# Moving one expert tile into the embedding, and small sums from VectorE to GpSimd, in a fused vision-tower layer

## The chip, the cores and the metric

The kernel runs on one core of a Trainium2 chip. The metric is the device time of one execution in microseconds (us). TensorE is called PE in the profile, VectorE DVE, ScalarE ACT, GpSimd POOL, and SyncE, which only issues transfers here, SP.

## The reference

The input x has the shape 4 x 64 x 512 x 64 (batch, channel, time, variable). Three stages follow each other; all is float32.

```python
# tokenizer: windows of 16 steps, stride 8, a real FFT of each, one linear layer
patches = xp[:, :, idx, :]                          # 64 windows of each variable
xf = rfft(patches, norm='ortho')
h = concat(xf.real, xf.imag) @ W.T                  # 4 x 4096 tokens of width 256

# retention layer on norm(h)
t = layernorm(h)
u = layernorm(t, g1, b1)
q, k, v = u @ Wq.T + bq, u @ Wk.T + bk, u @ Wv.T + bv
mem_t = decay * mem_{t-1} + k_t * v_t               # along the 4096 tokens
r = t + q * mem
h = h + r + (relu(layernorm(r, g2, b2) @ W1.T + b1) @ W2.T + b2)

# mixture of experts on norm(h): 8 experts, the best 2 for each token
t = layernorm(h)
p = softmax(t @ router.T); the two largest, scaled to sum 1, are the weights
h = h + t + sum over the chosen e of weight_e * (gelu(t @ w1[e] + b1[e]) @ w2[e] + b2[e])
```

## The kernel before, in words

**Blocks.** The 16,384 tokens are 32 blocks of 512 (four times 128). The main loop runs over blocks i from 0 to 30 and works on three of them at once: `new` is block i (embedding, q, k, v, retention), `mid` is block i-1 (the layer's MLP, whose 1024 columns are eight tiles of 128), `old` is block i-2 (router, scattering of its rows to the experts). The last block is treated after the loop.

**Order.** On TensorE, VectorE, ScalarE and SP the instructions stand in the order in which the program's text makes them; a step that is written earlier is queued earlier. GpSimd's order is left to the framework's scheduler. [...]

**The embedding** (`embed`, a generator that the loop advances by `next`) takes five products of differences of x. Products 1 and 2 go to one PSUM tile, which ScalarE copies to `ab` (line 423). Products 3 and 0 share another, and VectorE combines both into the four rows of `h` (line 420). Product 4 completes the last row. Statistics follow, GpSimd computes the norm's factors `rstd` (lines 288 to 293) by powers, and VectorE applies them (`zz`, line 297). `add_offsets` adds the MLP's second bias to `h` on GpSimd (line 454); `sum_up` adds the retention's result `z` to `h` on VectorE (line 648). `first_norm` makes `z` on ScalarE (line 459).

**Turning a block.** [...]From block 6 on a block is turned by a transfer: its floats are split into two 16-bit halves (`planes`, two ScalarE copies, line 330), SP issues a transposing transfer (`turned` or `turned_first`, line 340), and four copies join the halves to `hT` (line 349). In the earlier blocks TensorE transposes `zz` instead (line 310). `split1` and `features1` do this for the first norm, `split2` and `features2` for the norm before the MLP, `turn3` and `join3` for the router's tokens.

**Seven products for eight.** From block 7 on the MLP's two-by-two products are made of seven smaller ones with mixed sums of the input (`mix_normed`, `mix_tokens`; VectorE, lines 536 to 539). `mlp_group` works in steps between which the loop puts other work; three groups go in turn and the fourth, `rest`, later. q, k and v (`products`, called by `qkv`) are made in the same way from block 1 on: a first round of products, ScalarE copies into the fixed PSUM tiles `sums`, then rounds that add to them.

**Expert tiles.** Rows that go to one expert are collected in tiles of 256. A tile has six steps: `load` and `weigh` (SP fetches rows and the expert's weights, 641 KB), `turn` (two ScalarE copies to `xT`, line 1075), `enter` (first product, line 1082, and gelu, line 1090), `leave` (second product, line 1099), `sums` (VectorE adds the bias and scales, GpSimd adds the rows to the output in DRAM by two indirect transfers, line 1128). In each slot one tile enters and the tile before it leaves. Weights have four buffers, the PSUM pool `tm` has three, handed out in turn; a product into `tm` waits until the buffer of three uses before has been read. Four tiles run in a block of the steady part.

**Retention and residual.** `scan` multiplies k by v (line 614), runs the recurrence (line 615) and multiplies by q (`ret`, line 625). `residual` turns `ret` back on TensorE (line 636), adds it to `z` (line 639), takes statistics and computes the next norm's factors on VectorE in `factors_here`: an estimate by bits and three rounds of three small instructions (lines 276 to 282). The result, `zz`, is what `split2` splits.

**Routing.** `choose` finds both experts of each token, `place` counts the destinations and computes the row weights (`weights`), `scatter` sends the rows by eight indirect transfers on GpSimd (line 888); the later ones wait for given products of TensorE. `take` then lists the full tiles in some 21 tiny VectorE instructions; it stands between the request of the MLP norm's factors on GpSimd and their use in `tok`.

Of the kernel before, what the change touches and what calls it, by code (L numbers as in the profile page):

```python
# [12 lines left out]
F32 = mybir.dt.float32  # L13
# [23 lines left out]
def vit_tower_kernel(  # L37
# [160 lines left out]
    taken = const.tile([P, E], F32)  # L198
    nc.gpsimd.memset(taken, 0.0)
# [121 lines left out]
    class Turn:  # L321
# [5 lines left out]
        def split_steps(self, src, name="turned"):  # L327
            planes = one.tile([P, TT, 2 * D], U16, name="planes")
            for i, half in enumerate(halves(src)):
                nc.scalar.copy(planes[:, :, i * D : (i + 1) * D], half)  # L330
                if i:
                    self.start([planes.rearrange("p t d -> p (t d)")], name)
                yield
# [34 lines left out]
    class Block:  # L368
# [34 lines left out]
        def embed(self):  # L403
# [32 lines left out]
            scaled(h[3], c, 4.0 / 3, q, ALU.subtract)  # L436
            for t in range(TT - 1):
                norm.stats(self.h, t)
# [14 lines left out]
        def add_offsets(self):  # L453
            nc.gpsimd.tensor_tensor(self.h, self.h, mb2_sb.unsqueeze(1).to_broadcast([P, TT, D]), ALU.add)  # L454
# [86 lines left out]
        def products(self, which, first, to, order):  # L541
# [15 lines left out]
            def half(n):  # L557
                src = g[:, n, :]
# [6 lines left out]
            else:  # L565
                ps = p_tm.tile([P, 2, HALF], F32, name="tm")
            nc.tensor.matmul(ps[:, 0, :], lhsT=w11, rhs=a[:, :HALF], start=True, stop=True)
            nc.tensor.matmul(ps[:, 1, :], lhsT=t1, rhs=s1, start=True, stop=True)
            nc.scalar.copy(g, ps[:, 0:1, :].to_broadcast([P, 2, HALF]))
            p5 = three.tile([P, HALF], F32, name="p5")  # L570
            biased(p5, ps[:, 1, :], 1)
            yield
            add(0, w21, b[:, :HALF])
            add(1, t2, s2)
            biased(*half(0), 0)
# [15 lines left out]
            biased(*half(1), 0)  # L591
# [55 lines left out]
        def sum_up(self):  # L647
            nc.vector.tensor_tensor(self.h, self.h, self.z, ALU.add)

# [189 lines left out]

        def weights(self, diff, second):  # L840
# [19 lines left out]
        def place(self, at_once=True):  # L860
# [16 lines left out]
            self.weights(self.row.bitcast(F32)[:, :, DIFF], self.row.bitcast(F32)[:, :, SECOND])  # L877
# [49 lines left out]
    def take(n, block, writes):  # L927
# [5 lines left out]
        nc.vector.tensor_tensor(full, cnt, first[:, :E], ALU.subtract)  # L933
        if n == NS:
            nc.vector.tensor_scalar(full, full, float(S - 1), None, ALU.add)
        whole = small.tile([P, E], I32, name="whole")
        nc.vector.tensor_copy(whole, full)
        nc.vector.tensor_scalar(whole, whole, S.bit_length() - 1, None, ALU.arith_shift_right)
        nc.vector.tensor_copy(full, whole)

        nc.vector.tensor_tensor(full, full, taken, ALU.subtract)
        upto = small.tile([P, E + 1], F32, name="upto")
        nc.vector.memset(upto[:, 0:1], 0.0)
        nc.vector.tensor_tensor_scan(upto[:, 1:], ones_e, full, 0.0, ALU.mult, ALU.add)

        base = small.tile([P, E + 1], F32, name="base")
        nc.vector.tensor_tensor(base[:, :E], taken, upto[:, :E], ALU.subtract)
        nc.vector.tensor_scalar(base[:, E:], upto[:, E:], -1.0, None, ALU.mult)
        nc.vector.scalar_tensor_tensor(base, base, float(S), first, ALU.mult, ALU.add)

        shape = [P, k, E]
        past = one.tile([P, KMAX, E], F32, name="past")[:, :k, :]
# [7 lines left out]
        def along(to, of):  # L960

            step = small.tile([P, E], F32, name="step")
            nc.vector.tensor_tensor(step, of[:, 1:], of[:, :E], ALU.subtract)
            steps = one.tile([P, KMAX, E], F32, name="steps")[:, :k, :]
            nc.vector.tensor_tensor(steps, past, step.unsqueeze(1).to_broadcast(shape), ALU.mult)
# [10 lines left out]
        along(row, base)  # L976
        nc.vector.scalar_tensor_tensor(row, tile_f[:, :k], float(S), row, ALU.mult, ALU.add)
        done = None
        if n < NS:
            nc.vector.tensor_scalar(table[:, 1, :], row, base[:, 0:1], None, ALU.add)  # L980
# [606 lines left out]
```

## Time and profile before

| what | value |
|---|---|
| median of three runs | 2175.86 us (2172.4 to 2176.06) |
| the profiled execution, span | 2172.28 us, 2170.5 us |
| TensorE busy | 2075.3 us (96%) |
| VectorE busy | 1752.8 us (81%) |
| ScalarE busy | 1203.7 us (55%) |
| GpSimd busy | 963.1 us (44%) |
| steady block, embedding to embedding | some 63.4 us (1523.75 to 1587.16 is one) |
| granted TensorE clock, mean | 0.993 |

The profile comes from one execution. A line of its timeline has the start in us from the span's beginning, the duration in us, engine, source line, operation, tiles written and read, shapes, and in brackets the idle time of the engine before it and what ended it. A line of the waits names who waited for whom: us in total, times, longest us. PE and PEld are TensorE's products and its weight loads, which run beside each other; the end of a product is modelled. An fp32 product of 256 columns shows as two instructions.

### The profile page before, as it was taken

The numbers are of one execution on the slowest core, as the hardware profiler recorded it, in microseconds if no ns is written. First come the engines' busy times: TensorE is split into PE (matmuls) and PEld (weight loads), VectorE is DVE, ScalarE is ACT, GpSimd is POOL, SyncE is SP. The second block draws the span as 40 slices with busy tenths as digits, with TensorE's granted clock in tenths as the row PEclk, the third lists the DMA queues.
The fourth block names the chain that finished last, engine by engine and source line by source line (L and its number), as shares of the span: only waits on it lengthen the run. The fifth ranks groups of instructions, "written<-read, shape, count | busy, mean of one in ns | idle before, by whom it ended". The sixth has DMA issues, their size and how long they took to land.

```text
span 2170.5 us, 32402 instructions
## 1 busy us (share of the span) xinstructions
PE 2075.3 (96%) x9618; PEld 1671.4 (77%) x9618; DVE 1752.8 (81%) x5344; ACT 1203.7 (55%) x2350; POOL 963.1 (44%) x800
## 2 busy tenths in 40 slices
PE   8999999999999999999999999999999999899998
PEld 5776677877888777788877788887778888776776
DVE  7778888888888888888888888888888889768554
ACT  2344445765555675555567555556655556643443
POOL 1133334444455444445544444454445455335444
PEclk9999999999999999999999999999999999999999
DMA  4032246666576666567676656667665675768653
GB/s 138 8 116 65 84 107 135 133 146 135 127 159 145 151 125 149 132 137 158 145 150 127 146 127 146 157 141 153 128 145 129 146 157 139 137 173 197 104 74 49
DMA packets 424529, 283.32 MB, mean 131 GB/s; under 512 B 355104, under 2 KB 391072, under 8 KB 420256
## 3 DMA queue, kind: packets, MB, share of 16 engines
q1 hardware_dynamic: 373424, 208.35, 41.6%
q0 software_dynamic: 49632, 67.39, 17.0%
q10 hardware_dynamic: 1296, 5.52, 0.8%
q8 instruction: 75, 1.23, 0.2%
q14 instruction: 102, 0.84, 0.1%
HBM read 118.36 MB, written 86.52 MB: 94 GB/s over the span
## 4 chain that ended last, share of the span: by engine, by line
PE 44%; DVE 27%; DMA 11%; ACT 7%; issue 5%; POOL 4%; POOLq 0%; DVEq 0%; SPq 0%; ACTq 0%
PE tm L716 11%; PE sums L552 8%; PE mm L1082 6%; PE sums L357 6%; DMA turned<-planes 4%; DMA turned_first<-planes 4%; PE tm L1099 4%; DVE st L268 4%; DVE h L420 3%; ACT planes L330 3%; PE tm L414 2%; DVE zz L297 2%; ACT hT L349 2%; DMA out<-y,xg 2%; POOL rstd L293 2%
## 5 line engine op out<-in xcount | busy, mean ns | idle before, releaser
L1128 POOL DMA_INDIRECT out<-y,xg x226 | 387.5, 1715 | 441.8 <-DVE y L1118 217.4
L716 PE MATMUL tm<-w_sb,aT 128*128 128x256 f32 x2048 | 455.7, 381 | 0.0
L716 PEld LDWEIGHTS tm<-w_sb,aT 128*128 128x128 f32 x2048 | 388.2, 191 | 57.2 <-DVE z L639 4.6
L888 POOL DMA_INDIRECT xbuf<-row,to x248 | 262.1, 1057 | 169.2 <-DVE ks L588 88.9
L330 ACT COPY planes<-zz 128x1024 uint16<-128x1024 uint16 x100 | 99.6, 1042 | 341.9 <-DVE zz L297 299.3
L1099 PE MATMUL tm<-w,ge 128*128 128x256 f32 x1008 | 248.2, 390 | 36.2 <-ACT ab L423 36.2
L414 PE MATMUL tm<-wu,xv 128*128 128x256 f32 x1280 | 282.5, 379 | 0.0
L414 PEld LDWEIGHTS tm<-wu,xv 128*128 128x128 f32 x1280 | 242.7, 190 | 32.7
L1082 PE MATMUL mm<-xT,w 128*128 128x256 f32 x1008 | 241.9, 383 | 6.6 <-ACT xT L1075 4.5
L1099 PEld LDWEIGHTS tm<-w,ge 128*128 128x128 f32 x1008 | 187.8, 192 | 74.7 <-ACT ab L423 45.5
L288 POOL TENSOR_SCALAR rstd<-mv 128x4 f32<-128x4 f32 x62 | 42.0, 677 | 435.1 <-DVE mv L269 396.7
L1082 PEld LDWEIGHTS mm<-xT,w 128*128 128x128 f32 x1008 | 192.8, 192 | 37.1 <-ACT xT L1075 5.6
L1075 ACT COPY xT<-xh 128x512 uint16<-128x512 uint16 x262 | 181.7, 765 | 21.2 <-DMA xh<-xbuf 14.8
L1090 ACT ACTIVATE ge<-mm,w 128x256 f32<-128x256 f32 x252 | 105.5, 473 | 102.4 <-PE mm L1082 81.3
L349 ACT COPY hT<-turned 128x512 uint16<-128x512 uint16 x100 | 65.9, 757 | 141.9 <-DMA turned<-planes 141.9
L1116 DVE TENSOR_TENSOR y<-tm,w 128x512 f32<-128x512 f32 x126 | 87.1, 691 | 50.3 <-PE tm L1099 46.9
L357 PE MATMUL sums<-hT,w_sb 128*128 128x512 f32 x256 | 112.8, 592 | 0.0
L389 DVE TENSOR_TENSOR xv<-xb 128x512 f32<-128x512 f32 x160 | 104.2, 684 | 4.1 <-DMA xb<-in_x 4.1
L268 DVE BATCH_NORM_STATS2 st<-h 128x6 f32<-128x256 f32 x256 | 104.8, 409 | 3.3
L552 PE MATMUL sums<-hT,wqkv_sb 128*128 128x256 f32 x360 | 107.1, 379 | 0.0
L454 POOL TENSOR_TENSOR h<-h,mb_sb 128x1024 f32<-128x1024 f32 x32 | 90.7, 2835 | 23.9 <-ACT z L459 23.8
L297 DVE TENSOR_SCALAR zz<-h,mv,rstd 128x256 f32<-128x256 f32 x128 | 44.2, 409 | 67.2 <-POOL rstd L293 67.2
(265 smaller groups left out, 4168.1 us busy)
## 6 DMA issues: line engine op xcount, KB each, us to landing
w<-in_wex SPq DMA_DIRECT2D x111, 641.5 KB
xb<-in_x SPq DMA_DIRECT2D x32, 1040.0 KB
out<-h SPq DMA_DIRECT2D x31, 512.0 KB
bank<-in_wex ACTq DMA_DIRECT2D x8, 641.5 KB
xbuf<-row,to POOLq DMA_INDIRECT x248, 2.5
out<-y,xg POOLq DMA_INDIRECT x226, 5.5
xh<-xbuf SPq DMA_TRANSPOSE x131
xg<-xbuf SPq DMA_DIRECT2D x131, 4.0 KB
```

Source lines behind the costliest of these rows:

```text
L268: nc.vector.bn_stats(self.st[:, t, :], src[:, t, :])
L330: nc.scalar.copy(planes[:, :, i * D : (i + 1) * D], half)
L349: copy(to[:, 1 - i], self.turned[:, :, i, k, :])
L357: nc.tensor.matmul(ps, lhsT=w[:, k, ts(m, P)], rhs=rhs[:, k, :], start=k == 0, stop=k == KD - 1)
L414: nc.tensor.matmul(ps[:, n, :], lhsT=xv[:, i, j, :], rhs=wu[:, i, j, :], start=j == 0, stop=j == J - 1)
L552: nc.tensor.matmul(g[:, n, :], lhsT=lhsT, rhs=rhs, start=False, stop=True, skip_group_check=True)
L716: last_product[0] = nc.tensor.matmul(ps[:, i, :], lhsT=self.aT[:, k, ts(u * 2 + i, P)], rhs=w2_sb[:, k, :], start=k == 0, stop=k == KH - 1,)
L888: write = nc.gpsimd.indirect_dma_start(out=xbuf, out_offset=bass.IndirectOffsetOnAxis(ap=self.to[:, c, t : t + 1], axis=0), in_=self.row[: ...
L1075: nc.scalar.copy(halves[:, :, :, 1 - i], self.xh[:, i * KD : (i + 1) * KD, :])
L1082: nc.tensor.matmul(ps[:, m, :], lhsT=self.w[:, k * D + m * P : k * D + (m + 1) * P], rhs=self.xT[:, k, :], start=k == 0, stop=k == KD - 1,)
L1099: last_product[0] = nc.tensor.matmul(ps[:, c, :], lhsT=self.ge[:, k, ts(c, P)], rhs=w[:, (2 + k) * D : (3 + k) * D], start=k == 0, stop=k ...
L1128: add = nc.gpsimd.indirect_dma_start(out=out, out_offset=bass.IndirectOffsetOnAxis(ap=number[:, c, :], axis=0), in_=y[:, c, :], in_offset= ...
```

## The change

It reorders the loop's steps and moves some small work between engines:

- In blocks from 7 on, one tile's `enter` stands between the embedding's first two products and the next two, and the other tile's `leave` after these; `features2` follows the tile's entry. Before, the tile stood behind the whole embedding, and `features2` ahead of it. `split1` moves ahead of the last step of three MLP groups, the third tile's entry ahead of the fourth group's third step.
- `h + z` moves from VectorE to GpSimd, into `add_offsets`, which is called in the next block's pass, behind its embedding. For the last two blocks both sums are on VectorE.
- The row weights of `place` move to GpSimd (a power in place of the reciprocal).
- `take` has five fewer VectorE instructions: rounding by adding and subtracting a large number takes the place of two conversions and a shift.
- The first norm's split has one half on VectorE and one on ScalarE.
- The first round of q, k and v copies half as much, and its second round adds to the first product in place.
- `weigh` follows each tile's `sums` at once (`summed`); `turn` of a tile moves to other places.

The core of the diff:

```diff
@@ const
-    taken = const.tile([P, E], F32)
-    nc.gpsimd.memset(taken, 0.0)
...
+    nc.gpsimd.tensor_scalar(lower, first[:, :E], 1.0 / S, (S - 1) / (2.0 * S), ALU.mult, ALU.add)
+    minus = const.tile([P, TT], F32)
+    nc.gpsimd.memset(minus, -1.0)
@@ Turn.split_steps
-                nc.scalar.copy(planes[:, :, i * D : (i + 1) * D], half)
+                copy = nc.scalar.copy if i or name == "turned" else nc.vector.tensor_copy
+                copy(planes[:, :, i * D : (i + 1) * D], half)
@@ Block.add_offsets, sum_up
         def add_offsets(self):
+            nc.gpsimd.tensor_tensor(self.h, self.h, self.z, ALU.add)
             nc.gpsimd.tensor_tensor(self.h, self.h, mb2_sb.unsqueeze(1).to_broadcast([P, TT, D]), ALU.add)
...
         def sum_up(self):
             nc.vector.tensor_tensor(self.h, self.h, self.z, ALU.add)
+            nc.vector.tensor_tensor(self.h, self.h, mb2_sb.unsqueeze(1).to_broadcast([P, TT, D]), ALU.add)
@@ Block.products (q, k, v)
-            nc.tensor.matmul(ps[:, 0, :], lhsT=w11, rhs=a[:, :HALF], start=True, stop=True)
             nc.tensor.matmul(ps[:, 1, :], lhsT=t1, rhs=s1, start=True, stop=True)
-            nc.scalar.copy(g, ps[:, 0:1, :].to_broadcast([P, 2, HALF]))
+            nc.tensor.matmul(ps[:, 0, :], lhsT=w11, rhs=a[:, :HALF], start=True, stop=True)
             p5 = three.tile([P, HALF], F32, name="p5")
             biased(p5, ps[:, 1, :], 1)
+            nc.scalar.copy(g[:, 1, :], ps[:, 0, :])
             yield
-            add(0, w21, b[:, :HALF])
             add(1, t2, s2)
-            biased(*half(0), 0)
+            nc.tensor.matmul(ps[:, 0, :], lhsT=w21, rhs=b[:, :HALF], start=False, stop=True, skip_group_check=True)
+            biased(*half(0, ps), 0)
             nc.scalar.copy(g[:, 0, :], g[:, 1, :])
@@ Block.weights_there, called by place
+            share = small.tile([P, TT], F32, name="share")
+            nc.gpsimd.tensor_scalar(share, self.ex, 1.0, None, ALU.add)
+            nc.gpsimd.tensor_tensor(share, share, minus, ALU.pow)
+            nc.gpsimd.tensor_tensor(second, share, self.ex, ALU.mult)
+            nc.gpsimd.tensor_tensor(diff, share, second, ALU.subtract)
@@ take
-        nc.vector.tensor_tensor(full, cnt, first[:, :E], ALU.subtract)
+        nc.vector.scalar_tensor_tensor(full, cnt, 1.0 / S, lower, ALU.mult, ALU.subtract)
...
-        nc.vector.tensor_copy(whole, full)
-        nc.vector.tensor_scalar(whole, whole, S.bit_length() - 1, None, ALU.arith_shift_right)
-        nc.vector.tensor_copy(full, whole)
-
-        nc.vector.tensor_tensor(full, full, taken, ALU.subtract)
...
+        nc.vector.tensor_scalar(full, full, ROUND, None, ALU.add)
+        nc.vector.scalar_tensor_tensor(full, full, ROUND, taken, ALU.subtract, ALU.subtract)
@@ new helper
+    def summed():
+        advance("sums", at["leave"])
+        advance("weigh", at["leave"] + 4 + len(spare))
@@ main loop, start of a block's pass
-            embed = new.embed()
-            if seven:
-                mid.features2()
-                advance("turn", min(at["enter"] + 2, at["load"]))
-            next(embed)
-            if seven:
-                mid.mix_normed()
-            elif i > 1:
+            embed = new.embed(seven)
+            next(embed)
+            if i > 1 and not seven:
+                mid.features2()
+            tile_steps = iter(())
+            if seven:
+                tile_steps = slot_halves(known, load=False, turn=0, further=1, sums=False)
+                next(tile_steps, None)
                 mid.features2()
             if old:
                 old.rows()
                 old.turn3()
             next(embed)
+            if seven:
+                run(tile_steps)
+                mid.mix_normed()
+                next(embed)
...
-            if mid:
-                mid.sum_up()
+            summed()
...
             next(embed, None)
-            if at["enter"]:
-                slot(known, load=False, further=seven, sums=not seven)
+            if mid:
+                mid.add_offsets()
+            if at["enter"] and not seven:
+                slot(known, load=False)
@@ main loop, MLP groups, blocks from 7 on
-                for _ in range(3):
+                for n in range(3):
+                    if n == 2:
+                        advance("turn", min(at["enter"] + 2, at["load"]))
+                        new.split1()
...
-                new.split1()
-                next(tokens)
...
                 new.features1()
                 new.mix_tokens()
+                tile_steps = slot_halves(known, sums=False, turn=0)
+                next(tile_steps, None)
+                next(rest)
                 old.logits()
-                next(rest)
-                advance("sums", at["leave"])
@@ main loop, q, k, v (blocks from 7 on: the tile leaves between the first and the second round)
-                run(chain(rest, *groups[:3]))
+                run(rest)
+                if seven:
+                    old.choose()
+                next(qkv)
+                run(chain(*groups[:3]))
                 if i >= EARLY:
                     run(ahead)
-                next(qkv)
-                tile_steps = slot_halves(known, sums=False)
-                next(tile_steps, None)
+                run(tile_steps)
                 next(qkv)
                 if old:
                     writes = old.place(at_once=False)
                     old.scatter(1)
-                run(tile_steps)
-                if old:
                     old.scatter(2, last_product[0])
...
                 new.first_norm()
-                new.add_offsets()
@@ main loop, end of a block's pass
+            if i == NS - 1:
+                slot(known)
+            if at["enter"]:
+                advance("weigh", at["enter"] + AHEAD - 2)
+                advance("load", at["enter"] + AHEAD - 1)
...
                 new.split2()
+                summed()
```

## The prediction

> **What bounds the kernel now.** I read the page's engine totals first, then who waited for whom on TensorE, then the timeline of one repeating block (1450 to 1514 us), then that of an early block.
>
> ```profile
> PE 2075.3 (96%) x9618; PEld 1671.4 (77%) x9618; DVE 1752.8 (81%) x5344; ACT 1203.7 (55%) x2350; POOL 963.1 (44%) x800
> ```
>
> TensorE (PE) is the bound: only its stalls can be won. From the 256-column products' usual distance from start to start (216 ns, and likewise for the other shapes) I count some 180 us of stalls in all, weight loads made late after a wait included. The waits name the largest:
>
> ```profile
> PE tm L1099 <- ACT ab L423: 36.2, 23, 3.3
> PE tm L636 <- DVE ret L625: 10.9, 6, 2.4
> PE tm L676 <- DVE h L420: 6.2, 22, 0.3
> PE sums L676 <- ACT sums L689: 5.5, 24, 0.3
> PE sums L552 <- DVE ks L588: 3.9, 4, 2.7
> PE mm L1082 <- DMA w<-in_wex: 2.1, 1, 2.1
> ```
>
> The first happens once in each block from the seventh on. The timeline shows how:
>
> ```profile
> 1454.10 0.67 DVE L639 TENSOR_TENSOR z<-tm,z 128x512 f32<-128x512 f32 x1
> ...
> 1456.88 0.17 DVE L280 TENSOR_TENSOR st<-rstd 128x4 f32<-128x4 f32 x1
> 1456.97 0.97 POOL L888 DMA_INDIRECT xbuf<-row,to  x1 [0.30 <-issue]
> ...
> 1458.67 1.38 DVE L297 TENSOR_SCALAR zz<-z,mv,rstd 128x256 f32<-128x256 f32 x4
> ...
> 1460.09 1.99 ACT L330 COPY planes<-zz 128x1024 uint16<-128x1024 uint16 x2 [11.95 <-DVE zz L297]
> ...
> 1461.68 1.61 POOL L1128 DMA_INDIRECT out<-y,xg  x1 [3.74 <-DVE y L1118]
> ...
> 1467.67 2.63 ACT L349 COPY hT<-turned 128x512 uint16<-128x512 uint16 x4 [5.60 <-DMA turned<-planes]
> ...
> 1471.41 0.57 ACT L423 COPY ab<-tm 128x512 f32<-128x512 f32 x1
> 1472.01 0.76 DVE L420 SCALAR_TENSOR_TENSOR h<-ab 128x256 f32<-128x256 f32 x2 [3.52 <-ACT ab L423]
> ...
> 1472.04 1.99 PE L1099 MATMUL tm<-w,ge 128*128 128x256 f32 x8 [1.46 <-ACT ab L423]
> ```
>
> Read it as one chain: the residual's norm ends (zz, 1460.05), ScalarE splits it, a DMA turns it, ScalarE joins it (hT, 1470.3), and behind that in ScalarE's order stand two xT copies and ab, although ab's products were long done. The tile's second product waits for ab's PSUM buffer. I measure from R1, the first transpose of ret (1450.30): the embedding starts at R1+9.75, zz ends at R1+9.75, and G, the first MLP group product (L676), comes at R1+23.57. G to the next R1 takes 40.1 us; a block takes 63.5 (mean of 21).
>
> An early block shows what large work on GpSimd (POOL) does to VectorE (DVE):
>
> ```profile
> 192.83 3.68 DVE L615 TENSOR_TENSOR_SCAN ks<-vec,carry,kv 128x512 f32<-128x512 f32 x1
> 193.07 2.35 POOL L454 TENSOR_TENSOR h<-h,mb_sb 128x1024 f32<-128x1024 f32 x1
> ...
> 197.72 0.98 PE L636 MATMUL tm<-ident,ret 128*128 128x128 f32 x7 [1.68 <-DVE ret L625]
> ```
>
> The scan's median is 1.28 us. Under GpSimd's addition it took 3.68, and R1's transposes waited 1.68 for it. Statistics and additions from PSUM under the same addition kept their times.
>
> [...]the scan above, and L625 at up to 3.40 us against a median of 1.09. [...]Here 2.35 us unblocked against 1.19 for the same size on VectorE (L648)[...].
>
> **The change part by part**, in a block from the seventh on.
>
> *First tile inside the embedding.* TensorE's order becomes: products (1,2), tile's first product, products (3,0), tile's second, product 4. ab moves ahead of hT. TensorE's work from the embedding's start is unchanged, 8.64+1.73+1.73 = 12.1 us, so it could be at G by R1+21.85, 1.72 sooner. The MLP group in the tm pool then takes a buffer long empty: the 0.45 us wait for h L420, 0.59 with the late weight load, goes.
>
> *Sums on GpSimd.* h+z leaves VectorE (1.19 us) for GpSimd, together with h+mb. In the built program's order both stand on GpSimd behind the block's eight scatters, released by the second z addition (R1+4.47), not at the place the text suggests; ahead of the two output additions and the MLP norm's factors. The last two pairs of scatters, 0.98 us each and 0.3 apart, wait for TensorE at R1+0.2 and R1+3.0, so they end at R1+5.3. Then h+z runs to 7.65 and h+mb to 10.1. VectorE reaches L280, the first of nine small instructions with two SBUF inputs, at R1+6.58. [...]one or two pass between the two additions; the other seven, 0.2 us each, follow after about 9.95. So zz starts at R1+11.4, not 8.37: **3.0 us later** on the chain that decides G. No trace shows these small ones against such an addition: [...]I take 3.0, because the large ones waited in full.
>
> From zz's end to G VectorE now sets the time: the last tile's sums 1.53, MLP output and statistics 1.81; the factors on GpSimd, behind two output additions, let tok start 6.62 after zz (16 steps of choice end at 6.4, so their saving of 0.65 us is hidden); tok and by 1.7, embedding 0.76+1.86, first mix 0.45: 11.4 in all. G comes at R1+9.75+3.0+11.45 = 24.2, **0.65 later** than before. (By the DMA it would be 10.7 after zz.)
>
> *G to R1.* Gone: 0.59 above; 0.60 at the fourth group's third step (wait for L689), because a tile's first product now stands before it; 0.28 at its second; 0.45 for mixed tokens, because the first norm's split ends about 1 us sooner (one half on VectorE, estimate 0.9, the other on ScalarE, 1.04); 0.4 at the third steps behind VectorE. New: no tile lies between the second and third round of q, k, v, so these meet ScalarE's six copies (2.6 us against 2.6 us of products): 0.5. The next tile's xT stands behind them: 0.5. Small late weight loads: 0.4. Sum −2.32+1.4 = **−0.93**. VectorE reaches ret at G+39.1, as TensorE does, so no new wait there.
>
> *At no cost.* Row weights on GpSimd: at most 2.0+0.8+1.7+0.9+0.9 us from the exponential on, which ends as the destinations are ready; cover gone, the scatters start late, and their readers are a block away. First q, k, v copies halved (0.58 to 0.40): on ScalarE beside products. Weights and rows are fetched sooner on SP; ahead of turned stand one xh and xg, in the 11.95 us in which SP's next item waits for ScalarE. If that room were gone, 1.7 us. Fewer steps of choice hide behind the factors; without that cover they would save 0.65.
>
> *Elsewhere.* In early blocks GpSimd's addition no longer meets the scan: five R1 waits of 1.7 go. But zz 2.3 to 3.0 late passes its slack of 2.0 before the transposes of zz: 0.8 comes back. 5 x −0.9 = −4.5. Block 30: the row weights waited 3.49 on the exponential and TensorE 2.65 behind them, and 2.06 for weights now fetched sooner: −4.7, of which I take 4.
>
> Sum: 24 x 0.65 = +15.6; 24 x −0.93 = −22.3; −4.5; −4: **−15**. The profiled execution took 2172.3 (span 2170.5), at the low end of runs with median 2175.9; −15 gives 2157, and I forecast 2158.
>
> **Rivals.**
> [...](small instructions pass, or the additions fall in a gap). For it: no such pair in the trace. Against: every large pair. zz is on time, G comes at R1+21.9: 24 x (−1.67−0.93) = −62, −4.5, −4: 2172−70 = 2102; with half of the tail's gain, 2113.
> *GpSimd's additions come still later: slower.* If the scatters end at R1+6.8 instead of 5.3, all nine small steps lie behind both additions: zz 4.5 late, +1.5 in 24 blocks, +36−15: 2193. It decides from zz 3.6 us late on, where +0.6 a block eats the 15. For it: [...](h+mb took 2.93 behind ret, not 2.35). Against: VectorE has no two-input instruction between R1+0.2 and R1+6.58.
> *The turning DMA decides G anyway.* Then fewer steps and an early ab cannot help there: G at R1+23.5, 24 x (−0.07−0.93) = −24, −8.5: 2140. It lies between the first two.
>
> **How the numbers follow.** About 0.2%, 4 us, is what a measurement of this kernel can tell from no change. Likeliest case: 0.50, own range 2140 to 2180; 0.40 of it faster, 0.07 same, 0.03 slower. Lock without effect or DMA-bound: 0.22, faster. Additions later: 0.28, of it 0.03 same and 0.25 slower. Faster 0.62, same 0.10, slower 0.28. The range, 2105 to 2192, reaches into both rivals.
>
> **What would show it.** Right: h+z and h+mb at R1+5 to 10; an L280 or L281 of about 1 to 2.5 us in each block (their line in the changed file differs); zz ending near R1+12.8; G near R1+24.2, waiting for VectorE's mix; no wait for ab; early waits for ret gone; G to R1 near 39.2. Wrong: small instructions of unchanged length under the additions and zz at R1+9.75 (first rival); zz after R1+13.4 (second); waits of over 1 us in q, k, v or at xT, which the sum doesn't hold.

## The result, and the profile after

The changed kernel takes 2188.39 us (median of 8 runs, 2180.68 to 2195.33) against 2175.96 (8 runs, 2168.29 to 2177.63) for the kernel before on the same chip: a ratio of 1.0064, with a 95% interval of [1.0039, 1.0089]. It is slower; I had forecast 2158. The profiled execution took 2182.47 us (span 2180.7, before 2170.5).

The page's engine totals, after:

```profile
PE 2067.1 (95%) x9618; PEld 1699.1 (78%) x9618; DVE 1813.3 (83%) x5072; ACT 1173.4 (54%) x2325; POOL 1068.6 (49%) x953
```

VectorE has 272 instructions fewer than before and is busy 60 us longer. That is the first sign: some of its instructions wait while they count as busy (L287 below stands at 2.15 us, against 0.17 alone). The waits on TensorE, after (engine, line, who was waited for: us in total, times, longest):

```profile
PE mm L692 <- DVE kv L551: 67.9, 24, 4.5
PE mm L321 <- DVE zz L308: 9.9, 6, 4.0
PE mm L582 <- DVE planes L551: 9.9, 10, 1.8
```

The wait for ab (36.2 us) is gone, and of those of the early blocks for ret (10.9) 0.3 is left, as predicted. In their place G, the first MLP product (L692 here), waits for VectorE's first mix in 24 blocks, 2.8 us each. Where that comes from shows in the timelines. First the start of the residual's norm in the kernel before, with a scatter that runs beside it (R1 at 1450.30):

```profile
1455.70 0.96 POOL L888 DMA_INDIRECT xbuf<-row,to  x1 [0.30 <-issue]
1456.02 0.17 DVE L276 TENSOR_SCALAR mv<-mv 128x4 f32<-128x4 f32 x1
1456.22 0.42 DVE L277 TENSOR_SCALAR rstd<-mv 128x4 int32<-128x4 int32 x1
1456.67 0.17 DVE L278 TENSOR_SCALAR rstd<-rstd 128x4 int32<-128x4 int32 x1
```

Then one block of the changed kernel (R1 at 1460.49), where these three steps are L287 to L289:

```profile
1465.97 2.36 POOL L468 TENSOR_TENSOR h<-h,z 128x1024 f32<-128x1024 f32 x1
...
1466.22 2.15 DVE L287 TENSOR_SCALAR mv<-mv 128x4 f32<-128x4 f32 x1
1468.40 0.17 DVE L288 TENSOR_SCALAR rstd<-mv 128x4 int32<-128x4 int32 x1
1468.41 2.37 POOL L469 TENSOR_TENSOR h<-h,mb_sb 128x1024 f32<-128x1024 f32 x1
1468.61 2.20 DVE L289 TENSOR_SCALAR rstd<-rstd 128x4 int32<-128x4 int32 x1
...
1472.64 1.39 DVE L308 TENSOR_SCALAR zz<-z,mv,rstd 128x256 f32<-128x256 f32 x4
...
1481.72 2.62 ACT L361 COPY hT<-turned 128x512 uint16<-128x512 uint16 x4 [3.17 <-DMA turned<-planes]
...
1484.49 0.41 DVE L551 TENSOR_TENSOR kv<-hT 128x256 f32<-128x256 f32 x1
1484.96 0.70 PE L692 MATMUL mm<-kv,w_mix 128*128 128x256 f32 x2 [2.46 <-DVE kv L551]
```

Two steps of 0.17 us each, L287 and L289, become 2.15 and 2.20: each ends within 0.04 us of the end of one of GpSimd's additions. Only L288 passes between the two. (In 4 of the 23 periods below the additions start 1 us later; there L288 and L291 are held and zz starts near R1+13.) So zz starts at R1+12.15, not at R1+8.4 as before, and everything behind it in the chain (split, transfer, join, mix) is late. TensorE, which is at the end of the embedding by R1+22.0, waits until R1+24.5.

Means over the 23 periods from the R1 of block 6 to that of block 29 (numbered from 0), in us:

| | before | predicted | after |
|---|---|---|---|
| zz starts, behind R1 | 8.38 | +3.0 | 12.30 (+3.9) |
| G, behind R1 | 23.83 | +0.65 | 24.96 (+1.13) |
| G to the next R1 | 39.74 | −0.93 | 39.16 (−0.58) |
| period | 63.57 | −0.28 | 64.11 (+0.54) |

TensorE's clock shows something that the sum didn't hold. The windows view of the same block of the changed kernel (window, its length, PE busy, granted clock, DMA share, GB/s):

```profile
1480.40:1484.90 4.50, 2.10 (x10) 1.00 0.83 192
1486.30:1489.70 3.40, 3.40 (x10) 0.51 0.38 77
1489.70:1493.00 3.30, 3.30 (x16) 0.99 0.39 80
```

The wait ahead of G is followed by 3.4 us at half the clock, 1.7 us of work lost. That happens in 13 of the 23 periods, and the mean clock falls from 0.993 to 0.984. The periods can be compared with each other. In 15 of them the wait is 2.46 to 2.66 us long; 7 of these waits are followed by the half clock and 8 are not, and G to R1 takes 39.5 us in the former and 38.7 in the latter. So about half of the lost 1.7 us lengthens the period.

### The profile page after: what moved, and what is told of

It is laid out like the page before. It is cut to its first block, busy times and chain, and to the rows that moved or that the text cites. A ratio compares the mean times of both kernels' runs of the same rounds, so it can differ in the third digit from the quotient of the medians.

```text
span 2180.7 us, 32319 instructions
## 1 busy us (share of the span) xinstructions
PE 2067.1 (95%) x9618; PEld 1699.1 (78%) x9618; DVE 1813.3 (83%) x5072; ACT 1173.4 (54%) x2325; POOL 1068.6 (49%) x953
## 4 chain that ended last, share of the span: by engine, by line
PE 58%; DVE 27%; DMA 6%; issue 3%; POOL 3%; ACT 1%; SPq 0%; another core or an unknown queue 0%; POOLq 0%; ACTq 0%; DVEq 0%
PE tm L732 10%; PE sums L567 7%; PE mm L1102 7%; PE sums L692 6%; PE tm L1119 5%; PE sums L369 5%; PE mm L692 5%; DVE st L279 4%; DMA turned_first<-planes 4%; DVE rstd L289 3%; DVE mv L287 2%; DVE h L432 2%; DVE z L654 2%; PE tm L692 2%; DVE zz L308 2%
## 5 line engine op out<-in xcount | busy, mean ns | idle before, releaser
L1148 POOL DMA_INDIRECT out<-y,xg x226 | 377.0, 1668 | 387.6 <-DVE y L1138 218.6
L426 PE MATMUL tm<-wu,xv 128*128 128x256 f32 x1280 | 292.8, 381 | 1.3 <-DVE y L1136 1.3
L342 ACT COPY planes<-zz 128x1024 uint16<-128x1024 uint16 x75 | 75.8, 1042 | 362.9 <-DVE zz L308 360.1
L1119 PE MATMUL tm<-w,ge 128*128 128x256 f32 x1008 | 240.8, 382 | 0.0
L1119 PEld LDWEIGHTS tm<-w,ge 128*128 128x128 f32 x1008 | 189.4, 190 | 30.9 <-issue 1.9
L299 POOL TENSOR_SCALAR rstd<-mv 128x4 f32<-128x4 f32 x62 | 15.3, 247 | 304.6 <-DVE mv L280 277.1
L692 PE MATMUL mm<-kv,w_mix 128*128 128x256 f32 x144 | 52.6, 452 | 67.9 <-DVE kv L551 67.9
L692 PE MATMUL mm<-hT,w_sb 128*128 128x256 f32 x288 | 95.3, 416 | 0.0
L468 POOL TENSOR_TENSOR h<-h,z 128x1024 f32<-128x1024 f32 x30 | 70.8, 2360 | 47.8 <-DVE z L654 47.1
```

Source lines behind the costliest of these rows:

```text
L426: nc.tensor.matmul(ps[:, n, :], lhsT=xv[:, i, j, :], rhs=wu[:, i, j, :], start=j == 0, stop=j == J - 1)
L692: nc.tensor.matmul(dst, lhsT=lhsT, rhs=rhs, start=start, stop=True, skip_group_check=True)
L1119: last_product[0] = nc.tensor.matmul(ps[:, c, :], lhsT=self.ge[:, k, ts(c, P)], rhs=w[:, (2 + k) * D : (3 + k) * D], start=k == 0, stop=k ...
L1148: add = nc.gpsimd.indirect_dma_start(out=out, out_offset=bass.IndirectOffsetOnAxis(ap=number[:, c, :], axis=0), in_=y[:, c, :], in_offset= ...
```

## The experiments

All times are medians; a ratio is to the kernel before, run beside it on the same chip (2175.2 to 2177.5 us), with its 95% interval.

**e1: h+z back on VectorE, the bias addition back behind `first_norm`.**

```diff
-            nc.gpsimd.tensor_tensor(self.h, self.h, self.z, ALU.add)
...
             summed()
+            if mid:
+                mid.sum_up()
...
                 new.first_norm()
+                new.add_offsets()
```

No addition of GpSimd lies beside the residual's norm here, where two steps took 2.15 and 2.20 us in the changed kernel.

> The changed kernel with both sums put back: h+z on VectorE behind the embedding, h+mb on GpSimd behind the first norm, as in the kernel before; all else as changed. Theory ([...]TensorE's long wait before G halves its clock for 3.4 us or more): the norm's zz starts at R1+8.2 to 8.4 again, G comes near R1+22.0 without a wait of over 0.3 us, no clock loss in steady blocks, G to R1 37.8 to 38.4, a block of about 60 us: 2085 to 2110 us. Rival 1 (the additions only delay G, the clock is no part of it): G's wait of 2.6 us goes in 24 blocks, G to R1 stays 39.4: about 2120. Rival 2 (the loss comes from the order of tile and embedding, not from the sums): 2160 or more.

Measured: 2114.91, ratio 0.9708 [0.9681, 0.9735], a little above the expected interval. The move of the sums alone turned a gain of 61 us into a loss of 12. In the block below, L287 to L289 take 0.20, 0.17 and 0.17 us. What keeps it above the interval is the bias addition, which now meets ret (e5 takes it away). Timeline of this kernel:

```profile
1466.77 2.93 POOL L468 TENSOR_TENSOR h<-h,mb_sb 128x1024 f32<-128x1024 f32 x1
1467.14 3.50 DVE L639 TENSOR_TENSOR ret<-ret,ks 128x512 f32<-128x512 f32 x1
1468.38 0.27 PE L650 MATMUL tm<-ident,ret 128*128 128x128 f32 x1
...
1470.69 1.75 PE L650 MATMUL tm<-ident,ret 128*128 128x128 f32 x7 [2.04 <-DVE ret L639]
```

L639 takes 1.1 us alone and 3.50 here; the transposes of R1 stop for 2.04 after the first. In all, 27 waits cost 51.6 us.

**e2: the kernel before, with only the sums moved.** `add_offsets` gets h+z and stands behind the embedding, as in the change.

```diff
         def add_offsets(self):
+            nc.gpsimd.tensor_tensor(self.h, self.h, self.z, ALU.add)
...
-            if mid:
-                mid.sum_up()
...
             next(embed, None)
+            if mid:
+                mid.add_offsets()
...
-                new.add_offsets()
```

> The kernel before with only the sums moved to GpSimd (h+z and h+mb in add_offsets, called behind the next block's embedding). Theory: zz 3.8 us later in each block; there the copy ab and all behind it hang on hT, so each of 24 blocks is 3.8 us longer, and the longer idle time of TensorE lowers its clock: 2176 + 91, and up to 36 more by the clock: 2250 to 2305 us. Rival (the sums do no harm by themselves, or help since VectorE has 1.2 us less): 2165 to 2185.

Measured: 2293.57, ratio 1.0511 [1.0475, 1.0548]. zz starts at R1+12.14, and G comes at R1+29.1. The delay isn't cut short here: ab stands behind hT in ScalarE's order, so TensorE's wait for ab grows from 36.2 to 93.4 us. The clock is half for 6.8 us in 22 of the 23 periods (mean 0.959), and G comes 5.3 us later where zz comes 3.8 later. Together with e1 this leaves little doubt: the sums cost, the rest of the change gains.

**e3: the wait filled with work.** The embedding's fifth product is made twice.

```diff
-            nc.vector.tensor_tensor(h[3], products((4,))[:, 0, :], h[3], ALU.add)
+            nc.vector.tensor_tensor(h[3], products((4, 4) if apart else (4,))[:, 0, :], h[3], ALU.add)
```

> The changed kernel with four more matmuls (8 records, 1.73 us) behind product 4 of the embedding in blocks from 7 on: product 4 is made twice, its second copy goes to an unused half of its PSUM tile. They lie in the wait before G. Theory (the wait costs TensorE its clock besides): G stays at R1+24.6, the idle stretch shrinks from 2.6 to 0.9 us, the halved stretches behind G go, G to R1 falls from 39.4 to about 38 in the blocks that had them: 2160 to 2175 us, faster than the changed kernel by 12 to 28. Rival (no cost by the clock): as the changed kernel, 2183 to 2195, or slower if the products do not fit the wait (up to +41).

Measured: 2190.57, ratio 1.0052 [1.0033, 1.0071]; a miss. The wait ahead of G fell from 2.85 to 1.2 us in the mean and the half clock came in 4 periods of 23 instead of 13, yet G to R1 stayed at 39.34. The waits on TensorE in this kernel:

```profile
PE mm L582 <- DVE planes L551: 30.9, 21, 2.5
PE mm L692 <- DVE kv L551: 28.7, 24, 2.8
```

The first product of q, k, v (L582) now waits for the first norm's mixed tokens 30.9 us instead of 9.9. These follow G's mix on VectorE at a nearly fixed distance: embedding norm, split, transfer, join, mix, 17.7 to 20 us. A TensorE at full speed reaches L582 before they are ready; one that has lost 1.7 us comes about when they are. So part of the lost clock hid a second wait on the same chain. And the half clock follows that wait too: in 3 of the 4 periods it stands behind a wait at L582 of 1.8 to 2.3 us, and G to R1 takes 41.3 to 41.7 there. The filling moved the loss rather than removed it, and it doesn't measure what the clock costs; the comparison of periods above does.

**e4: one addition instead of two.** The bias is left out on GpSimd (blocks 0 to 29).

```diff
-            nc.gpsimd.tensor_tensor(self.h, self.h, mb2_sb.unsqueeze(1).to_broadcast([P, TT, D]), ALU.add)
```

> The changed kernel without the addition of the MLP's second bias on GpSimd (that bias is left out for the first 30 blocks); h+z stays there. Theory: [...]L287 waits until R1+7.8, the other small steps follow without a wait, zz starts near R1+10.3 (not 12.15), G near R1+22.8, TensorE idle before it under 1 us, no clock loss, G to R1 near 38: a block of 60.8 us, 2095 to 2120 us. Rival (the delay grows in proportion and the clock is no part of it): half of the wait stays, 1.3 us in 24 blocks: about 2150.

Measured: 2125.75, ratio 0.9768 [0.9736, 0.98]. zz at R1+10.1 and G at R1+22.4 to 22.6 in most blocks, as expected: one addition less brings zz forward by 2.05 us. The time is some 6 us above the interval because G to R1 is 39.4, not 38: the mixed tokens again (29.9 us in 22 waits), and the half clock in 5 of 23 periods.

**e5: no large addition on GpSimd.** Both sums on VectorE, from block 7 on behind the first norm's split, before that behind the embedding.

```diff
-            if mid:
-                mid.add_offsets()
+            if mid and not seven:
+                mid.sum_up()
...
+                mid.sum_up()
                 tokens = old.join3_steps(nc.scalar.copy)
```

> The changed kernel with both sums (h+z and h plus the MLP bias) on VectorE, behind the first norm's split; GpSimd makes no large addition. Theory (the block's length is a loop from R1 over zz, the MLP mix and the first norm to q, k, v and R1 again, and any instruction of VectorE that waits for GpSimd's addition lengthens it): against the version with h+z back on VectorE (2115), the 27 waits of R1 on ret, 1.9 us each, go; zz starts at R1+8.3 in every block; period 59.5 to 60.3; 2060 to 2085. Rival (VectorE is full already): the second addition's 1.2 us push the join of the first norm, q, k, v wait 0.5 to 1.2 us for mixed tokens in most blocks; 2085 to 2110. Rival (GpSimd's bias addition was hidden): 2110 or more.

Measured: 2069.98, ratio 0.9517 [0.95, 0.9533]. zz at R1+8.2, G at R1+21.9, no steady wait ahead of G, none for ret; period 60.0. The two sums on VectorE cost less than the waits they replace: it is busy 1761.0 us, 52 less than in the changed kernel, which had given h+z away. But from the first norm's split to its join VectorE is now full, and TensorE still waits 10.2 us in 25 waits for mixed tokens (see e8).

**e6: the first tile inside the embedding, alone, on the kernel before.**

```diff
-            embed = new.embed()
+            embed = new.embed(seven)
+            next(embed)
...
             if seven:
-                mid.features2()
-                advance("turn", min(at["enter"] + 2, at["load"]))
-            next(embed)
-            if seven:
-                mid.mix_normed()
-            elif i > 1:
+                tile_steps = slot_halves(known, load=False, turn=0, further=1, sums=False)
+                next(tile_steps, None)
                 mid.features2()
...
             next(embed)
+            if seven:
+                run(tile_steps)
+                mid.mix_normed()
+                next(embed)
```

> The kernel before with one part alone: the first expert tile inside the embedding's products and features2 behind its entry. Theory: the wait for ab (36 us in sum) goes, zz stays at R1+9.75 and its start at R1+8.4, G comes at R1+21.9 to 22.4, G to R1 39.2 to 39.8: period 61.3 to 62, 2115 to 2140. Rival (the turning transfer or VectorE's mix holds G where it was): G at R1+23.3 or later, 2150 to 2172. If it is slower than before, the reordering itself costs and the sums are not the whole cause.

Measured: 2158.67, ratio 0.9918 [0.9899, 0.9938]: a gain, but less than half of the expected one. The waits of this kernel on TensorE name the reason:

```profile
PE tm L638 <- DVE ret L627: 40.9, 21, 2.4
PE sums L678 <- ACT sums L686: 11.6, 24, 1.7
```

(The trace is of the fastest of the six runs, 2148.38 us.) As in e1, a faster TensorE brings R1 forward until the bias addition lies over ret. In the kernel before it lay just behind ret, from R1−0.3 on; that was the room that the reordering used up. In the 23 periods the price can be read: G stands at R1+21.84 without a wait for ret, at R1+23.95 with one of some 2.1 us, and at R1+25.6 in the 10 periods where the half clock follows that wait. Here nothing hides the lost 1.7 us. The second line, 0.5 us a block, is a cost of the new order itself; e9 has most of it too (10.5 us).

**e7: e5 with the row weights back on VectorE**.

```diff
-            self.weights_there(self.row.bitcast(F32)[:, :, DIFF], self.row.bitcast(F32)[:, :, SECOND])
+            self.weights(self.row.bitcast(F32)[:, :, DIFF], self.row.bitcast(F32)[:, :, SECOND])
```

> The version with both sums on VectorE, and the row weights back on VectorE (four small instructions of 0.2 us with a reciprocal instead of GpSimd's power). Theory that VectorE has no slack left ahead of ret: 0.4 to 0.9 us a block, 10 to 20 us slower than the version with both sums on VectorE. Theory of the prediction (this move is worth nothing): within 4 us of it.

Measured: 2071.87 (2070.65 to 2072.48) against 2069.98 (2068.5 to 2074.02): no difference that shows. The prediction's "at no cost" holds for this move: it neither costs nor gains here.

**e8: e5 with both halves of the first norm's split on ScalarE.**

```diff
-                copy = nc.scalar.copy if i or name == "turned" else nc.vector.tensor_copy
-                copy(planes[:, :, i * D : (i + 1) * D], half)
+                nc.scalar.copy(planes[:, :, i * D : (i + 1) * D], half)
```

> The version with both sums on VectorE, and both halves of the first norm's split on ScalarE, as before the change. Theory (the first norm is on the loop): the split ends some 0.9 us later, the first product of q, k, v waits 0.5 to 0.9 longer in each of 24 blocks, 12 to 22 us slower than the version with both sums on VectorE. Rival (TensorE has that much other work there): within 4 us of it.

Measured: 2060.56 (2055.55 to 2060.78), ratio 0.946 [0.944, 0.948]. Faster by 9 us, which neither theory had. The split ends 0.95 us later behind G, as expected (9.29 against 8.34 in most blocks), yet the join starts 0.5 sooner (15.31 against 15.84), and the waits for mixed tokens fall from 10.2 us to 0.8. The join doesn't wait for the split: it waits for VectorE. Timelines of VectorE, e5 and then e8:

```profile
1226.25 0.69 DVE L342 COPY planes<-zz 128x1024 uint16<-128x1024 uint16 x1
...
1234.79 0.62 DVE L1135 TENSOR_SCALAR y<-y,tile_share 128x256 f32<-128x256 f32 x2
1235.32 1.47 DVE L361 COPY hT<-turned_first 128x512 uint16<-128x512 uint16 x4
```

```profile
1227.99 0.61 DVE L1134 TENSOR_SCALAR y<-y,tile_share 128x256 f32<-128x256 f32 x2
1228.52 1.46 DVE L360 COPY hT<-turned_first 128x512 uint16<-128x512 uint16 x4
```

In nearly every block of both kernels VectorE has no idle time in the 7 us ahead of the join, which starts as y ends; and where the trace holds the landing of the transfer, it landed 0.3 to 2.3 us before the join in e5 and 0.5 to 1.5 before it in e8. So the transfer isn't what ends last. The half of the split that e5 has on VectorE (L342, 0.69 us) stands in this full stretch; without it the join comes 0.53 sooner. This is the fastest version of the study. Its engine totals:

```profile
PE 2027.2 (98%) x9618; PEld 1685.3 (82%) x9618; DVE 1746.7 (85%) x5107; ACT 1197.5 (58%) x2350; POOL 917.6 (45%) x893
```

**e9: e6 with both sums on VectorE, behind the first norm's split.**

```diff
-            nc.gpsimd.tensor_tensor(self.h, self.h, mb2_sb.unsqueeze(1).to_broadcast([P, TT, D]), ALU.add)
...
             nc.vector.tensor_tensor(self.h, self.h, self.z, ALU.add)
+            nc.vector.tensor_tensor(self.h, self.h, mb2_sb.unsqueeze(1).to_broadcast([P, TT, D]), ALU.add)
...
                 new.split1()
+                mid.sum_up()
```

> The kernel before with the first tile inside the embedding (as in the run of that part alone, 2159), and with both sums on VectorE behind the first norm's split, so that GpSimd makes no large addition. Theory (in the run of that part alone R1 came sooner and met GpSimd's bias addition: 21 waits on ret of 1.95 us and zz 1.9 us late): both go, G at R1+21.9, period 60.2 to 60.8, 2085 to 2110. Rival (VectorE, with 1.2 us more and the longer choice of tiles, is the bound): ret or mixed tokens late by about 1 us, 2115 to 2145. Rival (the reordering gains only what it gained alone): 2150 or more.

Measured: 2105.52, ratio 0.967 [0.9645, 0.9695]. The waits for ret are gone, G is at R1+21.9: what held e6 back was the bias addition's collision. The other parts of the change, less the split on two engines, make the further 45 us or so to e8, mostly between G and R1 (39.4 here, 37.65 there).

**e10: the kernel before with the same edit as e9, and nothing else.**

```diff
-            nc.gpsimd.tensor_tensor(self.h, self.h, mb2_sb.unsqueeze(1).to_broadcast([P, TT, D]), ALU.add)
...
             nc.vector.tensor_tensor(self.h, self.h, self.z, ALU.add)
+            nc.vector.tensor_tensor(self.h, self.h, mb2_sb.unsqueeze(1).to_broadcast([P, TT, D]), ALU.add)
...
                 new.split1()
+                mid.sum_up()
```

> The kernel before, with both sums on VectorE behind the first norm's split and no other change. Theory (in the kernel before, GpSimd's bias addition lies behind ret in blocks from 7 on and costs nothing there; only the early blocks' ret waits, 8 us, and the wait for ab stays): 2155 to 2176, period 63 to 63.6. Rival (the bias addition held G there too): 2140 or less. Rival (1.2 us more on VectorE cost): 2180 to 2205.

Measured: 2184.07, ratio 1.0034 [1.0023, 1.0045]; the last rival's range. The early blocks gain 7.4 us. In the others the join of the first norm comes late on VectorE, so TensorE waits for hT (16.5 us in 21 waits) and G to R1 grows by 1.0. In the old order the bias addition on GpSimd did hardly any harm after block 6 (without it G comes 0.2 us sooner); it did once TensorE was faster (e1, e6).

**e11: the sums on GpSimd, but later.** They wait for the first norm's split.

```diff
-            nc.gpsimd.tensor_tensor(self.h, self.h, self.z, ALU.add)
+            added = nc.gpsimd.tensor_tensor(self.h, self.h, self.z, ALU.add)
+            if behind is not None:
+                after(added, [behind])
...
                         new.split1()
+                        mid.add_offsets(new.turn.last)
```

> The changed kernel with both sums on GpSimd as they are, but made to wait for the first norm's split, so that they run some 10 us behind G instead of over the residual's norm. Theory (it is the place of the additions that costs, since small steps ahead of zz lie on the loop and those behind the split don't): zz back at R1+8.2, no wait ahead of G, a blocked xv of 2 to 4 us on VectorE instead, which has some 1.2 us of room plus the 1.2 that h+z took: 2065 to 2105. Rival (any place costs about the same, VectorE being nearly full): the join of the first norm comes 2 us late, q, k, v wait for it, 2115 to 2190.

Measured: 2137.26, ratio 0.9818 [0.9795, 0.9841]. zz is back at R1+8.2 and G at R1+21.9 (mean 21.96), as the theory had it, and 51 us of the loss are gone: that much was the place. But the time lies in the rival's range, 67 us behind e5. Of these, 17 lie ahead of R1 of block 6, where the edit changes nothing, and 50 in the 23 periods behind it, where the rival put them:

```profile
1648.79 2.84 POOL L468 TENSOR_TENSOR h<-h,z 128x1024 f32<-128x1024 f32 x1
1649.53 5.42 DVE L401 TENSOR_TENSOR xv<-xb 128x512 f32<-128x512 f32 x2
1651.71 2.69 POOL L471 TENSOR_TENSOR h<-h,mb_sb 128x1024 f32<-128x1024 f32 x1
...
1659.97 0.70 PE L584 MATMUL mm<-planes,wqkv_mix 128*128 128x256 f32 x2 [2.04 <-DVE planes L553]
```

Two instructions of 0.68 us take 5.42, the join behind them starts 1.8 us later than in e5, and TensorE waits 2.04 for the mixed tokens (51.8 us in 24 waits). As in e8, it is VectorE that brings the join late.

**e12: each sum cut into four instructions.**

```diff
-            nc.gpsimd.tensor_tensor(self.h, self.h, self.z, ALU.add)
+            for t in range(TT):
+                nc.gpsimd.tensor_tensor(self.h[:, t, :], self.h[:, t, :], self.z[:, t, :], ALU.add)
```

and the bias likewise.

> The changed kernel with each of GpSimd's two sums cut into four instructions of 128x256 (an estimated 0.6 us each, a quarter of 2.36), in the same place. They may also start earlier, since a quarter needs only its part of z. Theory A (GpSimd keeps VectorE out for the length of one instruction, and one small step of VectorE passes between two): steps such as L287 take up to 0.6 us instead of 2.2, but most of the eleven meet a piece; zz starts at R1+11 to 12.3 (changed kernel 12.15), G at R1+23.8 to 25, 2165 to 2190. Theory B (several small steps pass in each gap): zz at R1+9.5 to 10.5, G at R1+22.5 to 23, 2115 to 2150. Theory C (VectorE is kept out as long as GpSimd has additions queued): a step of 2 us or more still stands in each block, zz at R1+12 or later, 2185 to 2210.

Measured: 2197.07, ratio 1.0114 [1.0075, 1.0153]: theory C, in nearly all blocks. Timeline of this kernel:

```profile
1286.18 0.74 POOL L469 TENSOR_TENSOR h<-h,z 128x256 f32<-128x256 f32 x1
1286.33 0.64 DVE L293 SCALAR_TENSOR_TENSOR rstd<-st,rstd 128x4 f32<-128x4 f32 x1
1286.87 1.41 POOL L471 TENSOR_TENSOR h<-h,mb_sb 128x256 f32<-128x256 f32 x2
1287.00 4.02 DVE L291 TENSOR_TENSOR st<-rstd 128x4 f32<-128x4 f32 x1
1288.23 1.40 POOL L469 TENSOR_TENSOR h<-h,z 128x256 f32<-128x256 f32 x2
1289.60 1.40 POOL L471 TENSOR_TENSOR h<-h,mb_sb 128x256 f32<-128x256 f32 x2
```

L293 passes as one quarter gives way to the next; then one step (L291, 0.17 us alone) waits through the next six, 4.02 us. A step of 4.0 to 4.7 us stands in 28 of the 30 blocks. In blocks 0 and 1, though, the quarters follow each other just as closely, and four steps pass one by one, 0.53 to 0.65 us each, as theory A had it; zz starts at R1+10.4 and R1+9.9 there. What decides between the two isn't shown.

## Why the prediction was wrong

The mechanism was the one forecast: GpSimd's additions hold VectorE's small steps, zz is late, and G with it. Its size was wrong. The second rival's direction and nearly its number came (slower, 2193; it was to decide from zz 3.6 us late on), with 28 of 100 chances, but not for its reason: the additions did not come later, the first step was held earlier. That the rival's number fits is luck. By the steps of the prediction, the span's change of +10.2 is made of the following. (Its terms add up to +0.63 and −0.92 rather than +0.65 and −0.93, which moves the forecast by less than 1 us.)

| term of the sum | predicted | measured |
|---|---|---|
| G behind R1 | 24 x 0.65 = +15.6 | 23 x 1.13 = +25.9 |
| G to R1 | 24 x −0.93 = −22.3 | 23 x −0.58 = −13.4 |
| early blocks | −4.5 | +4.6 |
| block 29 to block 30 | −4 | −9.1 |
| start, and all behind block 30's period | 0 | −1.1, +3.2 |

- **"One or two pass between the two additions; the other seven follow": the step that failed.** The additions ran at R1+5.5 to 10.3, as forecast (5.3 to 10.1). But I let the waiting begin at L280, the first small step with two SBUF inputs (R1+6.58). It begins three places earlier, at L287 in the new file, with a single input, at R1+5.7. One step passes between, ten come after. So zz is 3.9 us late instead of 3.0: past the point where I had the sign change, and 10 of the 25 us between forecast and result by way of G. The 3.0 was an estimate: it took small steps to wait in full, as the scan did (3.68 us, median 1.28), and only those with two SBUF inputs, which no trace had shown. The trace shows two steps with one input that wait (2.15 and 2.20 us against 0.17). Other steps kept their times under a large addition: statistics (0.18 in both kernels), additions from PSUM (0.67 in the kernel before), a one-column copy (0.15 in e1).
- **The kernel before had shown it.** L277 takes 0.42 us there, against a median of 0.17, and ends as the scatter beside it does (1456.64 and 1456.66). Of the 102 records of L276 to L278, 28 are longer than 0.22 us, and 25 of these end 0.03 us before a scatter does. So GpSimd held small steps with one input there already, by its scatters.
- **VectorE's 11.4 us from zz's end to G** was nearly right: 11.3 in the mean of the 23 periods.
- **G to R1** was short of the forecast by 0.35, 9 of the 25 us. Two terms failed. The half clock stood nowhere in the sum: the periods without it have 38.7 us, which is 1.0 less than before and so about the forecast; the 13 with it have 39.5. And the "0.45 for mixed tokens, because the first norm's split ends about 1 us sooner" did not come: the split ends 1.8 us sooner behind G (9.6 against 11.4), but the join starts 0.9 later (16.7 against 15.8). In the 10 periods at full clock VectorE stands idle ahead of the join (0.3 to 2.4 us) and the transfer ends that wait: from its issue to the join it is 6.5 to 8.6 us there, 4.2 to 4.8 before. Its issue on SP now follows that of a 641 KB fetch of weights by 0.7 to 3.1 us in 22 of the 23 periods; before, the item ahead of it was some 7.6 us away. No run moved that fetch, so the reason stays open.
- **Early blocks.** I gave zz 2.0 us of slack and let 0.8 come back. The waits for ret did go, and the transposes of zz waited 0.8 to 1.1 us in four of the blocks 1 to 5, as forecast. But I left out block 0, whose transposes waited 2.4 and which grew by 3.4; and blocks 1 to 5 grew by 1.2 in all instead of losing 4.5. What makes these 6 us no run shows; in e5, without the additions, blocks 1 to 5 are 12 us shorter than before. Together this is another 9 of the 25 us.
- **Block 30** gained 9.1 where I had counted 4, and the part behind it gave 3.2 back; neither was followed up.
- **Right:** no wait for ab, no early wait for ret, h+z and h+mb in their places, the row weights at no cost (e7), and that TensorE could be at G by R1+21.85: with the sums gone from GpSimd it is there at R1+21.84 (e5, e8).

The change thus holds two parts of opposite sign: a reordering that brings 61 us (e1), and a move of the sums that costs 73 (the changed kernel against e1). With the bias addition off GpSimd as well, which was there before the change too, the reordering brings 105 (e5).

## What to carry to other kernels

An addition that leaves VectorE for GpSimd can still cost VectorE time: here 1.19 us were saved and 3.9 were lost, because two small steps beside it waited 2.2 us each. Before moving such work, list every VectorE instruction that will run beside it, also those with one input, and ask which lies on the chain that closes the block's loop. And when a part frees TensorE, look at what then slides under what: the bias addition that was harmless at R1−0.3 cost 1.9 us a block once R1 came earlier.

## What the runs showed of the hardware that I had not expected

- Steps of 128x4 elements with one input waited until GpSimd's addition ended (2.15 to 2.2 us instead of 0.17), and between two additions 0.08 us apart exactly one step passed, in all 30 blocks of the changed kernel. Between quarters without a gap one waited 4.0 us or more in 28 of 30 blocks, while in two blocks one passed after each (e12).
- Scatters from GpSimd held such steps too, in their later part: L277 took up to 0.43 us in the kernel before, against a median of 0.17. In 4 blocks of the changed kernel a step was held by a scatter and then by the addition behind it, 2.9 to 3.06 us.
- GpSimd's addition took 2.36 us where it came first in the changed kernel. It took 2.69 to 2.93 in the blocks shown where VectorE was at work with data from SBUF as it began (e11, e1), and 2.82 to 2.94 in 24 blocks of the kernel before with ret under way. That it waits for VectorE in its turn fits; but in the block at 1450 us ret had 0.28 us to go as an addition of 2.93 us began, so that isn't the whole account.
- The clock was halved for 3.4 us behind waits of some 2 us. Gaps of 2.46 to 4.5 us were followed by it in 13 of 23 periods, waits for ret of 2.0 to 2.2 us in 10 of 15 (e6) and in 3 of 20 (e1), and the shortest was 1.8 (e3). The same wait, 2.46 to 2.66 us in 15 periods of the changed kernel, was followed by it in 7 and not in 8; no run shows why.
